# A scan in two sweeps: silu as one ScalarE instruction, and the first sweep moved behind the attention

## The chip, the cores and the metric

The kernel runs on one core of one Trainium2 chip. The metric is the device time of one execution in microseconds (us), given as the median of the runs shown. Everything is computed in fp32.

## The reference

What is computed, cut to what matters (T = 4096 rows x, S2 = 3202 rows of context, H = 512, 8 heads of 64, NS = 64 states):

```python
x1 = x + mha(layernorm(x), layernorm(ctx))       # 8 heads, softmax over 3202 keys
U  = (layernorm(x1) @ W_in.T + b_in) @ Bmat      # 4096 x 64

def step(s, u_t):
    s = silu(s @ A.T) + u_t
    return (s, s)
states = scan(step, zeros(64), U)                # 4096 steps, each on the one before

out = x1 + states @ Cmat + mean(program_probs) @ W_prog.T + b_prog
```

## The kernel before, in words

**Attention.** The 4096 queries are cut into 8 blocks of 512, each into 4 pairs of heads and 2 halves: 64 units. A unit goes through its keys in 13 steps of up to 256 keys. One step is a group of 16 scores matmuls (`scores`, L647), one exponential on ScalarE (`weights`, L724), one sum for the denominators on VectorE (`add`, L732) and a group of 16 matmuls with the values (`product`, L781). At a unit's end a "join" on VectorE (L830) empties the accumulator `o`, so that the next unit's first product can start. `sample`, `maximum`, `spread` and `base` find each unit's softmax reference beforehand. When a block is through, `project` does its output projection, the second layernorm, the transposing moves by DMA on SyncE's queue (`move`, L1010) and the input projection `pu` (L1109), whose result is kept in the tile `u`, as A's input for all time steps.

**How 4096 dependent steps are done.** The time axis is cut into 256 chunks of L = 16 steps. They lie side by side: 128 chunks on the upper 64 partitions, 128 on the lower ones, so one instruction does one step of all chunks. A first sweep (prefix `a`, in the trace the tile `za`) starts every chunk at zero and gives each chunk's end state, `end1`. A second sweep (prefix `b`, tile `z`) starts every chunk from its predecessor's `end1`; its states are the result. At the end `differ` compares the second sweep's end states with those of the first (bound `TOL` = 2^-21 of the largest), the number of differences is cast to an integer (`nbad`, L1703), and if it isn't zero a general path computes everything again with as many sweeps as are needed. The last 256 rows are ready only after the last unit; their scan is a separate one with chunks of 4 steps and 16 steps of run-up (`last_rows`, 20 small steps, tile `zl`).

**One step of a sweep** is, for each chunk, `z = A h + A u` and `h = silu(z)`; the state is `s = h + u`. TensorE makes the products with `u` four time steps at a time (`terms`, L1245), and adds A times `h` onto them (`z_`). Silu is made of two instructions: ScalarE's tanh (L1271) and VectorE's `(tanh + 1) z` (L1278); A is halved and `u` doubled beforehand so that no further factor is needed. The second sweep's state is added by GpSimd (`states`, L1310), from there TensorE takes it into `products` (L1317, into `py`), and `outputs` adds them to the rows: one half of the row block by VectorE (`joined`, L1337), the other, in two steps of three, by a ScalarE copy (L1331) and an addition on GpSimd (L1334), in the third by VectorE as well.

```python
        def tanh_(j):
            nc.scalar.activation(sv["th"][j % 2], at_(j), AF.Tanh, scale=0.5)
        ...
            nc.vector.scalar_tensor_tensor(
                h, sv["th"][j % 2], 1.0, at_(j), ALU.add, ALU.mult
            )
```

**What sets the order.** Each engine executes its instructions in one order that the program writes out. A planner (`Plan`) makes it: each piece has an engine, a cost, the pieces that it comes after, a due time in steps of 2150 ns, and rings of buffers that it takes and gives. Of the pieces that are ready the one due first goes next; `SHIFT` moves the due times of single kinds of pieces by hand. The first sweep is due within the last unit's steps (its z matmuls stand between scores and product groups, its tanh between the exponentials), `A_PACE` 1500 ns apart; the second sweep is due in the drain after the last unit, `B_PACE` 1900 ns apart. `drain` adds all of it, the last output projection (`last_products`, L1398) and the comparison.

Of the kernel before, what the change touches and what calls it, by code (L numbers as in the profile page):

```python
# [38 lines left out]
NP = 18  # L39
TOL = 2.0**-21  # L40
# [27 lines left out]
class Plan:  # L68
# [114 lines left out]
def xattn_ssm_kernel(  # L183
# [54 lines left out]
    bu2 = const.tile([P, 1], F32, name="bu2")  # L238
# [172 lines left out]
    def side():  # L411
# [65 lines left out]
        for k in (0, NS):  # L477
            nc.vector.tensor_copy(bu[k : k + NS], pb[:NS, 0:1])
            nc.vector.tensor_scalar(bu2[k : k + NS], pb[:NS, 0:1], 2.0, None, ALU.mult)
# [12 lines left out]
        nc.vector.tensor_scalar(a_t, a_t, 0.5, None, ALU.mult)  # L492
# [297 lines left out]
    def sums(w):  # L790

        if w["last"]:
            w["pd"] = ps_s.tile([P, 2, 512], F32, tag="s", name="pd_last")[:, 0, :QU]
# [38 lines left out]
    def finish(w, i, d, plan):  # L832
# [62 lines left out]
        if last:  # L895
            plan.add(("rise", i), "DVE", 480, rise, inverses, d + 9000, [], [("s", ("sums", i))])
# [134 lines left out]
    def project(plan, Q, halves, d, index):  # L1031

        for half in halves:
# [81 lines left out]
            def kept(t, w=w, at=at):  # L1115
# [6 lines left out]
                    bias=bu2[of],  # L1122
                    scale=2.0,
# [59 lines left out]
    A_PACE, B_PACE = 1500, 1900  # L1183
# [32 lines left out]
    def open_scan():  # L1216
# [7 lines left out]
        sv["th"] = [one[:, i, :] for i in range(2)]  # L1224
        sv["h"] = [one[:, 2 + i, :] for i in range(3)]
        sv["s"] = [one[:, 5 + i, :] for i in range(2)]
# [3 lines left out]
        for name, n in (  # L1230
            ("end0", NCK + 1), ("end1", NCK + 1), ("ul", PRE + 1 + P), ("hw", P), ("hl", P),
            ("sl", P + 1), ("df", NCK), ("thl", P // LT), ("st", P // LT),
# [12 lines left out]
    def terms(z, q, start):  # L1245

        if q:
            on_a(z, u[:, 4 * q - 1 : 4 * q + 3, :], start=True)
            return
        if start is not None:  # L1250
            on_a(z[:, 0, :], start, start=True)
        on_a(z[:, 1:, :], u[:, :3, :], start=start is None)

    def sweep(k, start, end, d=0, pace=0, after=()):

        def bank(q):
            return sv["za" if k == "a" else "z"][q % 2]

        def at_(j):
            return bank(j // 4)[:, j % 4, :]

        def terms_(q):
            terms(bank(q), q, None if start is None else sv[start][:, :NCK])

        def z_(j):
            on_a(at_(j), sv["h"][(j - 1) % 3], start=False)

        def tanh_(j):  # L1270
            nc.scalar.activation(sv["th"][j % 2], at_(j), AF.Tanh, scale=0.5)  # L1271

        def h_(j):
            h = sv["h"][j % 3]
            if j == 0 and start is None:
                nc.vector.memset(h, 0.0)
                return
            nc.vector.scalar_tensor_tensor(  # L1278
                h, sv["th"][j % 2], 1.0, at_(j), ALU.add, ALU.mult
            )  # L1280

        def last_():
            e = sv[end]
            nc.vector.tensor_tensor(e[:, 1:], sv["h"][(L - 1) % 3], u[:, L - 1, :], ALU.add)
            nc.vector.tensor_copy(e[NS:, 0:1], e[:NS, NCK : NCK + 1])

        for j in range(L):
            q = j // 4
            if j % 4 == 0:

                free = [(k, "h", 4 * q - 5)] if q > 1 else list(after)
                yield (k, "terms", q), "PE", 880, partial(terms_, q), free, d - 3 * pace if q else d, [], [], "quarters"
            if j or start is not None:
                if j:
                    yield (k, "z", j), "PE", 250, partial(z_, j), [(k, "terms", q), (k, "h", j - 1)], d, [], [], "quarters"
                yield (
                    (k, "tanh", j), "ACT", 280, partial(tanh_, j),
                    [(k, "z", j) if j else (k, "terms", 0)], d + 400,
                )
                free = [("states", j - 3)] if j > 2 and start is not None else []  # L1300
                gives = [("m", "open")] if k == "a" and j == L - 1 else []
                yield (k, "h", j), "DVE", 290, partial(h_, j), [(k, "tanh", j)] + free, d + 800, [], gives
            else:
                yield (k, "h", j), "DVE", 100, partial(h_, j), [(k, "terms", 0)], d + 800
            d += pace
        yield (k, "end"), "DVE", 450, last_, [(k, "h", L - 1)], d

    def states(j, h):
        s = sv["s"][j % 2]
        nc.gpsimd.tensor_tensor(s, h, u[:, j, :], ALU.add)  # L1310
        return s
# [10 lines left out]
    def outputs(j):  # L1322

        n = counts[1]
        spread = j % 3 < 2
# [4 lines left out]
        def copied():  # L1330
            nc.scalar.activation(sv["y"][:, j % 2, :], sv["py"][j % 2][1], AF.Copy, scale=0.5)  # L1331
# [4 lines left out]
        def joined(v):  # L1336
            nc.vector.scalar_tensor_tensor(  # L1337
                row(v), sv["py"][j % 2][v][: counts[v]], 0.5, row(v), ALU.mult, ALU.add
# [32 lines left out]
    def first_scan():  # L1371

        sv["za"] = [m_tile([P, 4, NCK], f"za_{k}") for k in range(2)]
# [15 lines left out]

    def ready_py():  # L1390

        yb = ps_s.tile([P, 2, H], F32, tag="s", name="py")
        sv["py"] = [None, [yb[:, v, :] for v in range(2)]]
# [9 lines left out]
    def last_rows(plan, d):  # L1403
# [45 lines left out]
        def kept_(g):  # L1449
            hs = slice(g * NS, (g + 1) * NS)  # L1450
            nc.vector.tensor_scalar(
                sv["ul"][hs, PRE + 1 :], v["pu"][g][hs], bu[hs], 2.0, ALU.add, ALU.mult
            )
# [40 lines left out]
        for g in range(2):  # L1494
            plan.add(("last", NC - 1, g), "PE", 950, partial(last_products, NC - 1, [g]),
                     [("scale", n, g), ("last", NC - 2)], d + g)
# [9 lines left out]
            plan.add(("l.inputs", g), "PE", 1050, partial(inputs_, g), [("l.copy", g)], d + g, mt)  # L1506
# [5 lines left out]
        plan.add("l.terms", "PE", 1100, terms_, [("l.kept", g) for g in range(2)], d, ["mt"], [], "quarters")  # L1512
        for t in range(PRE + LT):
            if t:
                plan.add(("l.z", t), "PE", 150, partial(on_, t), [("l.h", t - 1)], d, [], [], "quarters")
            plan.add(("l.tanh", t), "ACT", 180, partial(tanh_, t), [("l.z", t) if t else "l.terms"], d)
            plan.add(("l.h", t), "DVE", 180, partial(h_, t), [("l.tanh", t)], d)
# [11 lines left out]
    def last_output(g):  # L1529
        nc.vector.scalar_tensor_tensor(  # L1530
            xl[g], sv["pyl", g], 0.5, xl[g], ALU.mult, ALU.add
# [4 lines left out]
    def neighbours():  # L1536

        sl = sv["sl"]
        nc.vector.tensor_copy(sl[:NS, 0:1], sv["end0"][NS:, END : END + 1])
# [65 lines left out]
    def drain(plan):  # L1605
# [15 lines left out]
        plan.add("open", "DVE", 600, first_scan, ["c2", ("den", n - 4, 1), *kept_], a0, ["m", "m"])  # L1621
        for p in sweep("a", None, "end1", a0 + 1000, A_PACE, ["open"]):
            plan.add(*p)
        plan.add("start", "SP", 0, ready_scan, ["fetch", ("sums", n)], d - 2 * STEP, ["s"])
        plan.add("yb", "SP", 0, ready_rows, [("den", n - 1, 1)], a0, ["m", "m"])
        plan.add("py1", "SP", 0, ready_py, ["start", ("rise", n)], d, ["s"])
# [331 lines left out]
```

## Time and profile before

| | |
|---|---|
| median of 3 runs | 1967.35 us (1966.62 to 1969.19) |
| the profiled execution | 1969.03 us |
| its span | 1967.2 us |
| its mean granted TensorE clock | 0.995 |
| TensorE (PE) busy | 1930.5 us, 98% of the span |
| VectorE (DVE) busy | 1460.4 us, 74% |
| ScalarE (ACT) busy | 1174.3 us, 60% |
| GpSimd (POOL) busy | 225.1 us, 11% |

The profile is one execution of the program recorded by the hardware. The span goes from its first instruction to its last; the device time of the same execution is 1.8 us longer. L1243 is line 1243 of the kernel's file; a name such as `za<-u` is the tile that is written and the tile that is read. A row of the timeline begins with its time in the span and its duration in us; in brackets stands how long the engine was idle ahead of it and which engine ended that.

### The profile page before, as it was taken

How to read it: one execution, taken by the hardware profiler on the slowest of the kernel's cores; microseconds unless marked ns; L12 is line 12 of the kernel's file. 1: busy time of each engine (PE TensorE's matmuls, PEld its weight loads, DVE VectorE, ACT ScalarE, POOL GpSimd, SP SyncE). 2: the span in 40 equal slices, each digit the busy share in tenths (PEclk: the TensorE clock that was granted, in tenths of full speed). 3: DMA queues.
4: the chain of work that ended last, by engine and by line, in shares of the span. 5: the costliest groups of instructions: out<-in, count | busy, mean ns of one | idle time of the engine just before them, and what ended most of it. 6: DMA issues, size and time to landing. Idle time of an engine off the chain costs nothing. (4 is left out here: it accounts for less than half of the span.)

```text
span 1967.2 us, 66894 instructions
## 1 busy us (share of the span) xinstructions
PE 1930.5 (98%) x29070; PEld 1256.5 (64%) x29070; DVE 1460.4 (74%) x1977; ACT 1174.3 (60%) x1632; POOL 225.1 (11%) x378
## 2 busy tenths in 40 slices
PE   8999999999999999999999999999999999999997
PEld 4444577676666666666667666666666676766674
DVE  4221289688877887788868886888788886877776
ACT  2233377576666566666657665666666675665653
POOL 2111000001200120001100120012001110011105
PEclk9999999999999999999999999999999999999998
DMA  5632323223432243233412342224322331544475
GB/s 171 192 98 72 98 81 99 70 80 91 125 87 80 77 121 76 72 94 80 116 57 88 91 123 78 80 85 117 89 77 74 102 91 47 150 135 141 146 206 196
DMA packets 246933, 204.27 MB, mean 104 GB/s; under 512 B 80808, under 2 KB 220072, under 8 KB 246636
## 3 DMA queue, kind: packets, MB, share of 16 engines
q1 hardware_dynamic: 242088, 192.28, 34.1%
q10 hardware_dynamic: 4548, 7.67, 1.2%
q8 instruction: 230, 3.77, 0.8%
q14 instruction: 67, 0.55, 0.1%
HBM read 156.32 MB, written 29.88 MB: 95 GB/s over the span
## 5 line engine op out<-in xcount | busy, mean ns | idle before, releaser
L724 ACT ACTIVATE p<-s,shifts 128x1024 f32<-128x1024 f32 (+1 forms) x832 | 891.1, 1082 | 487.4 <-PE s L647 477.5
L732 DVE TENSOR_TENSOR acc<-p,acc 128x1024 f32<-128x1024 f32 (+1 forms) x704 | 830.7, 1180 | 205.5 <-ACT p L724 171.2
L647 PE MATMUL s<-q,k 64*64 64x256 f32 x12800 | 835.3, 377 | 5.6 <-ACT p L724 3.7
L781 PE MATMUL po<-p,v 64*64 64x256 f32 x12800 | 834.9, 377 | 3.0 <-DVE o L830 2.4
L647 PEld LDWEIGHTS s<-q,k 64*64 64x64 f32 x12800 | 490.2, 133 | 218.8 <-issue 17.0
L781 PEld LDWEIGHTS po<-p,v 64*64 64x64 f32 x12800 | 484.6, 133 | 194.1 <-issue 12.9
L1047 POOL TENSOR_TENSOR xr<-xr,rowb 128x512 f32<-128x512 f32 x30 | 42.9, 1440 | 988.1 <-DMA xr<-in_x_dram 854.0
L853 DVE RECIPROCAL rd<-rd 128x256 f32<-128x256 f32 (+1 forms) x64 | 110.2, 1722 | 12.9 <-ACT rd L848 12.5
L324 PE MATMUL pq<-xn,wq 128*128 128x512 f32 x256 | 113.9, 598 | 0.0
L1053 PE MATMUL pa<-wo,o 128*128 128x512 f32 x240 | 107.0, 599 | 0.0
L563 PE MATMUL pv<-wv,ct 128*128 128x512 f32 (+1 forms) x208 | 95.6, 612 | 1.0 <-ACT ct L531 0.7
L596 PE MATMUL pk<-ct,wk 128*128 128x512 f32 (+1 forms) x224 | 88.8, 549 | 0.0
L531 DVE COPY ct<-tp_c 128x512 f32<-128x512 f32 (+1 forms) x13 | 8.5, 651 | 104.5 <-PE tp_c L295 104.5
L732 DVE TENSOR_TENSOR acc<-p,p 128x1024 f32<-128x1024 f32 x64 | 78.2, 1221 | 9.0 <-ACT p L724 9.0
L324 PEld LDWEIGHTS pq<-xn,wq 128*128 128x128 f32 x256 | 47.3, 190 | 57.9 <-issue 56.7
L1053 PEld LDWEIGHTS pa<-wo,o 128*128 128x128 f32 x240 | 44.4, 190 | 56.0 <-issue 55.5
L756 DVE TENSOR_TENSOR acc<-swap,acc 64x256 f32<-64x256 f32 x126 | 62.7, 498 | 11.1 <-ACT swap L751 9.4
L563 PEld LDWEIGHTS pv<-wv,ct 128*128 128x128 f32 (+1 forms) x208 | 38.1, 192 | 44.4 <-issue 42.2
L596 PEld LDWEIGHTS pk<-ct,wk 128*128 128x128 f32 x224 | 39.2, 190 | 42.6 <-issue 42.6
L333 ACT ACTIVATE q<-pq,bias 128x512 f32<-128x512 f32 x32 | 22.0, 687 | 73.4 <-PE pq L324 73.4
L604 ACT ACTIVATE ks<-pk,bias 128x512 f32<-128x512 f32 (+1 forms) x28 | 18.0, 642 | 75.5 <-PE pk L596 68.4
L751 ACT COPY swap<-acc 64x256 f32<-64x256 f32 x126 | 50.8, 403 | 17.2 <-DVE acc L739 14.5
(213 smaller groups left out, 1203.3 us busy)
## 6 DMA issues: line engine op xcount, KB each, us to landing
k<-kd SPq DMA_DIRECT2D x432, 128.0 KB, 2.3
v<-vd SPq DMA_DIRECT2D x432, 128.0 KB, 2.3
xn<-x SPq DMA_DIRECT2D x416, 32.0 KB, 1.9
xr<-in_x_dram SPq DMA_DIRECT2D x30, 256.0 KB, 3.2
x1d<-xr SPq DMA_DIRECT2D x30, 256.0 KB, 2.2
x<-in_x_dram SPq DMA_DIRECT2D x28, 256.0 KB, 3.4
cx<-in_ctx_dram SPq DMA_DIRECT2D x25, 256.0 KB, 2.9
vd<-vs SPq DMA_DIRECT2D x25, 256.0 KB, 2.4
```

Source lines behind the costliest of these rows:

```text
L324: nc.tensor.matmul(pq, wq[:, i, hp * P : (hp + 1) * P], xn[:, i, :], start=(i == 0), stop=(i == NC - 1),)
L563: nc.tensor.matmul(pv[h * HD : h * HD + n, :H], ct[:, k, o : o + n], wv[:, k, :], start=(i == 0), stop=(i == NC // parts - 1), skip_group_ ...
L596: nc.tensor.matmul(pk[:, :n_g], wk[:, i, hp * P : (hp + 1) * P], ct[:, i, :n_g], start=(i == 0), stop=(i == NC - 1),)
L647: nc.tensor.matmul(s[k0 : k0 + HD, a, b, :], kts[(*w["at"][:2], c)][r, b * CK + k0 : b * CK + k0 + HD], q[r], start=True, stop=True, skip_ ...
L724: nc.scalar.activation(t[:, :, :nb, :], w["ps"][c][:, :, :nb, :], AF.Exp, bias=w["shift"])
L732: nc.vector.tensor_tensor(w["acc"][:, :, :nb, :], t[:, :, :nb, :], before[:, :, :nb, :], ALU.add)
L751: nc.scalar.copy(w["swap"][r], of[(1 - k) * HD : (2 - k) * HD])
L756: nc.vector.tensor_tensor(of[r], w["swap"][r], of[r], ALU.add)
L781: nc.tensor.matmul(w["po"][a * HD : (a + 1) * HD, k, :QU], vts[Q, hp, c][r, b, a * HD : (a + 1) * HD], t[r, a, b, :], start=(c == 0 and b ...
L853: nc.vector.reciprocal(w["rd"][:, part], (w["pd"] if last else w["rd"])[:, part])
L1047: nc.gpsimd.tensor_tensor(v["x"], v["x"], rowb, ALU.add)
L1053: nc.tensor.matmul(v["pa"], o_t[Q, c, half][:, t * P : (t + 1) * P], wo[:, c, :], start=(c == 0), stop=(c == NC - 1),)
```

## The change

Both sweeps take silu from ScalarE's own function: no tanh, no product on VectorE, and so neither a halved A nor a doubled `u`. Exponential and silu are not in one table of ScalarE, so the whole first sweep is moved behind the last exponential, with one table load between them. The first sweep keeps its terms products. The second sweep has none: its matmuls take the state itself (`z = A s`), silu is done in place in PSUM, and VectorE adds `u`, which gives the state; GpSimd's additions of the states go. The states lie in a ring of `HS` = 5 tiles. The rows of the lower half are spread over ScalarE and GpSimd at every step, where it was two of three. The scan of the last rows takes silu in the same way. The last output products are split by row tiles, two tiles in PSUM are shared, and `SHIFT` has new values, for pieces of the attention too.

```diff
+HS = 5
...
     SHIFT = {
-        "row.store": 16.5, "fold": 6.75, "rows.outs": 1, "heads": -12.25, "sample": -3, "spread": 5.75,
-        "query.flip": 10.25, "states": -11.5, "inverse": 7.5, "extra": 4, "scale": -13.25, "rest": 3.25,
-        "row.mod": -1.5, "joined0": -6,
+        "row.store": 19.5, "fold": 9.5, "rows.outs": 0.75, "heads": -12.25, "query.flip": 8.75, "start": -18.25,
+        "row.mod": -28.25, "add": -1, "spread": -2.75, "fall": 14.25, "query.stats": -16.25, "row.move1": 12.25,
+        "extra": 2.5, "last": -2.5, "gather": 9.5, "rest": 2.75, "row.load": -2, "join": -9.75, "differ": -1,
+        "row.stats": -3.75, "b": -35.75, "l.out": 10.25, "joined0": -6,
     }
...
-        nc.vector.tensor_scalar(a_t, a_t, 0.5, None, ALU.mult)
...
-                    bias=bu2[of],
-                    scale=2.0,
+                    bias=bu[of],
...
-    A_PACE, B_PACE = 1500, 1900
+    A_PACE, B_PACE = 850, 1900
...
+    def first_sweep(d, pace, after):
         def terms_(q):
+            if q:
+                on_a(sv["z"][q % 2], u[:, 4 * q - 1 : 4 * q + 3, :], start=True)
+            else:
+                on_a(sv["z"][0][:, 1:, :], u[:, :3, :], start=True)
         def z_(j):
+            if j > 1:
+                on_a(at_(j), sv["h"][(j - 1) % 2], start=False)
...
+            nc.scalar.activation(sv["h"][j % 2], at_(j), AF.Silu)
...
+            old = [("a", "h", j - 1)] if j > 1 else [("weights", len(units) - 1, NDC - 1)]
...
+    def sweep(start, d=0, pace=0, after=(), waits=lambda j: []):
+        def z_(j):
+            on_a(at_(j), sv["s"][(j - 1) % HS] if j else sv[start][:, :NCK], start=True)
+        def h_(j):
+            nc.scalar.activation(at_(j), at_(j), AF.Silu)
+        def states_(j):
+            nc.vector.tensor_tensor(sv["s"][j % HS], at_(j), u[:, j, :], ALU.add)
         for j in range(L):
+            yield ("b", "z", j), "PE", 220, partial(z_, j), [("states", j - 1)] if j else list(after), d, [], [], "quarters"
+            yield ("b", "h", j), "ACT", 280, partial(h_, j), [("b", "z", j)], d + 400
+            yield ("states", j), "DVE", 290, partial(states_, j), [("b", "h", j)] + waits(j), d + 800
...
-    def states(j, h):
-        s = sv["s"][j % 2]
-        nc.gpsimd.tensor_tensor(s, h, u[:, j, :], ALU.add)
-        return s
...
-        spread = j % 3 < 2
+        spread = j % 16 < 16
...
-        def tanh_(t):
-            nc.scalar.activation(sv["thl"], z_(t), AF.Tanh, scale=0.5)
         def h_(t):
-            nc.vector.scalar_tensor_tensor(hs_(t), sv["thl"], 1.0, z_(t), ALU.add, ALU.mult)
+            nc.scalar.activation(hs_(t), z_(t), AF.Silu)
...
-            plan.add(("last", c), "PE", 1900, partial(last_products, c),
-                     ["yb"] + [("scale", i, t) for t in range(2) if ("scale", i, t) in plan.pieces] + ([("last", c - 1)] if c else []), d + 8 * STEP + c)
+            for g in range(2):
+                scaled = ("scale", i, g if ("scale", i, g) in plan.pieces else 0)
+                plan.add(("last", c, g), "PE", 950, partial(last_products, c, [g]),
+                         [scaled, ("last", c - 1, g) if c else "yb"], d + 8 * STEP + c + g / 2)
```

More of the change, by code (lines that the diff above doesn't have):

```diff
@@ L1243, in on_a, with at_ @@
             nc.tensor.matmul(z[r], a_t[r, r], right[r], stop=True, skip_group_check=True, **how)
[L1245 to L1262, printed above, removed]
+    def at_(j):
+        return sv["z"][j // 4 % 2][:, j % 4, :]
@@ L1273, in h_ @@
         def h_(j):
[L1274 to L1280, printed above, removed]
+            nc.scalar.activation(sv["h"][j % 2], at_(j), AF.Silu)
         def last_():
-            e = sv[end]
-            nc.vector.tensor_tensor(e[:, 1:], sv["h"][(L - 1) % 3], u[:, L - 1, :], ALU.add)
+            e = sv["end1"]
@@ L1285, in last_ @@
+            nc.vector.tensor_tensor(e[:, 1:], sv["h"][(L - 1) % 2], u[:, L - 1, :], ALU.add)
             nc.vector.tensor_copy(e[NS:, 0:1], e[:NS, NCK : NCK + 1])
-        for j in range(L):
[L1288 to L1304, printed above, removed]
-            d += pace
@@ L1306, in sweep @@
-        yield (k, "end"), "DVE", 450, last_, [(k, "h", L - 1)], d
-    def states(j, h):
-        s = sv["s"][j % 2]
-        nc.gpsimd.tensor_tensor(s, h, u[:, j, :], ALU.add)
-        return s
+        for j in range(1, L):
+            q = j // 4
+            if j == 1 or j % 4 == 0:
+                free = [("a", "h", 4 * q - 5)] if q > 1 else list(after)
+                yield ("a", "terms", q), "PE", 860 if q else 650, partial(terms_, q), free, d - 3 * pace, [], [], "quarters"
+            old = [("a", "h", j - 1)] if j > 1 else [("weights", len(units) - 1, NDC - 1)]
+            if j > 1:
+                yield ("a", "z", j), "PE", 220, partial(z_, j), [("a", "terms", q)] + old, d, [], [], "quarters"
+            yield (("a", "h", j), "ACT", 280 if j > 1 else 1580, partial(h_, j),
+                   [("a", "z", j)] if j > 1 else [("a", "terms", 0)] + old, d + 400)
+            d += pace
@@ L1637, in drain, with waits @@
         last_rows(plan, d - 16 * STEP)
-        for p in sweep("b", "end1", "end0", d - 9 * STEP, B_PACE, [("a", "end"), "start"]):
+        def waits(j):
+            return [("products", j - HS, part) for part in range(2)] if j >= HS else []
+        for p in sweep("end1", d - 9 * STEP, B_PACE, [("a", "end")], waits):
             plan.add(*p)
```

86 lines of the change are left out of this document (38 added, 48 removed).

## The prediction

> **What bounds the kernel now.** I read the page, then windows cut at the places where the work changes character, then the tiles of the first sweep, then the timeline of the tail.
>
> ```profile
> span 1967.2 us, 66894 instructions
> PE 1930.5 (98%) x29070; PEld 1256.5 (64%) x29070; DVE 1460.4 (74%) x1977; ACT 1174.3 (60%) x1632; POOL 225.1 (11%) x378
> ```
>
> ```profile
> 1814.00:1817.40 3.40, 2.99 (x28) 2.34 (x32) 0.00 (x0) 0.95 (x2) 0.00 (x0) 0.50 0.81 241
> ...
> 1850.00:1907.00 57.00, 54.91 (x965) 43.19 (x965) 42.17 (x62) 36.49 (x59) 3.49 (x2) 1.00 0.59 161
> ...
> 1920.00:1951.30 31.30, 27.00 (x404) 19.18 (x402) 20.69 (x59) 14.61 (x44) 21.98 (x32) 1.00 0.56 185
> 1951.30:1967.20 15.90, 5.88 (x70) 2.95 (x62) 10.69 (x34) 2.07 (x7) 3.50 (x4) 0.69 0.61 210
> ```
>
> Columns: window, length, busy of PE, PEld, DVE, ACT, POOL, granted clock, DMA share, GB/s. Up to the last exponential (about 1907) TensorE sets the time: whatever it stops doing there is won one for one. After that nothing is full: from 1920 to 1951 the second sweep runs as a chain through three engines, and from 1951 to the end PE is busy 5.9 of 15.9 us. There latency and queue order count, not busy time. The profiled execution took 1969.03 us, 1.8 more than its span and 1.7 more than the median of 1967.35; I add my sum to 1969.03 and take 1.7 off for the median. The measurement can't tell less than 0.2% (3.9 us) from no change.
>
> **Before the last exponential: the first sweep goes.**
>
> ```profile
> L1243 PE MATMUL za<-scan,a_t x60: 269/269/320, 1857.6 to 1899.1; 64*64 64x128 f32 x60
> ...
> L1243 PE MATMUL za<-u,a_t x16: 482/589/589, 1856.0 to 1881.1; 64*64 64x512 f32 x12, 64*64 64x384 f32 x4
> ...
>   PEld za L1243: 1.5, 3
> ```
>
> ```profile
> 1867.23 0.59 PE L1243 MATMUL za<-u,a_t 64*64 64x512 f32 x1
> ...
> 1868.73 0.40 PE L781 MATMUL po<-p,v 64*64 64x256 f32 x2
> ...
> 1870.73 1.21 PE L647 MATMUL s<-q,k 64*64 64x256 f32 x16
> ...
> 1872.46 1.21 PE L647 MATMUL s<-q,k 64*64 64x256 f32 x16
> ...
> 1874.40 1.21 PE L647 MATMUL s<-q,k 64*64 64x256 f32 x16
> ```
>
> A scores group and a product group together advance TensorE 1.73 us (1870.73 to 1872.46), 0.865 each; with one step of the first sweep between them 1.94. So a step costs 0.21, and 60 matmuls are 15 steps: 3.2 us. A set of terms: from 1867.23 to 1868.73 (1.50 us) 14 of 16 product matmuls went out, worth 0.76, so the terms took 0.74; four sets, one at three quarters width, 2.8 us. Waits of the weight loads for VectorE's product 1.5. Together 7.4 us leave the bound stretch.
>
> **Also before it: the planner's order shifts.** The new SHIFT values move instructions everywhere; the number of changes between full and quarter tiles on TensorE stays. Three places in the old order stall and stand differently in the new one.
>
> ```profile
> 849.07 1.09 PE L781 MATMUL po<-p,v 64*64 64x256 f32 x16 [1.10 <-DVE o L830]
> ...
> 1270.97 1.09 PE L781 MATMUL po<-p,v 64*64 64x256 f32 x16 [1.09 <-DVE o L830]
> ...
> 1814.41 1.98 PE L1109 MATMUL pu<-xn,wc 128*64 128x128 f32 x16 [3.29 <-DMA xn<-x]
> ...
> 1850.01 1.09 PE L1109 MATMUL pu<-xn,wc 128*64 128x128 f32 x16
> ```
>
> At 1811 the input projection of the block at row 3328 waits 3.29 us for its transposing moves, and then the clock is at 0.50 from 1814 to 1817.4: 2.99 busy us do 1.5 us of work (its 16 matmuls take 1.98 instead of 1.09). In the new order two scores groups and a product stand ahead of it, 3 x 0.865 = 2.6 us. On SP's queue the last of its four moves goes behind one more k load, one more v load and two row loads, but a k and a v load go ahead of the first move, into SP's idle time; I take the landing as unchanged. The stall shrinks to 0.7, and the half clock should go: 2.6 + 1.5 = 4.1 us won (bounds 0 and 4.8). The page "TensorE: Matmul & The Clock Gate" of the Trainium skill (Part 1) states that the clock halves after an idle window of about 3.4 us; the trace agrees, with 3.29 idle and 3.4 at half. By that rule 0.7 idle keeps the clock; if the halving came all the same, the place would give 2.6.
>
> At 849 and 1271 the next unit's first product waits for the join that empties its accumulator. In the new order 0.43 us more of other matmuls stand between, and the join is due 9.75 steps earlier on VectorE: 2.2 us won (bounds 0.9 and 2.2). Against that, the softmax maxima have less time: the least distance between sample and spread falls from 2.4 to 1.7 us of TensorE work at two places. No row prices that; between 0 and one more stall like that at 1811 (3.29 + 1.5), nearest to the 1.1 us rows, I take 1.5 lost. Sum up to the last exponential: -7.4 - 4.1 - 2.2 + 1.5 = -12.2 us.
>
> **After it: the first sweep comes back, serial.**
>
> ```profile
> 1906.62 0.70 ACT L724 ACTIVATE p<-s,shifts 128x512 f32<-128x512 f32 x1
> ...
> 1911.40 3.70 PE L1398 MATMUL yb<-wo,o 128*128 128x512 f32 x8
> ...
> 1916.05 3.77 PE L1398 MATMUL yb<-wo,o 128*128 128x512 f32 x8
> ...
> 1919.75 0.43 PE L1243 MATMUL z<-scan,a_t 64*64 64x128 f32 x4
> ...
> 1922.23 0.81 ACT L279 ACTIVATE xh_yl<-x_l,nmr_yl,rstd_yl 128x512 f32<-128x512 f32 x1 [0.15 <-POOL nmr_yl L271]
> ...
> 1922.62 0.43 PE L1243 MATMUL z<-scan,a_t 64*64 64x128 f32 x4 [0.93 <-DVE scan L1278]
> ...
> 1923.10 0.28 ACT L1271 ACTIVATE scan<-z 128x128 f32<-128x128 f32 x1
> 1923.41 0.29 DVE L1278 SCALAR_TENSOR_TENSOR scan<-scan,z 128x128 f32<-128x128 f32 x1 [0.85 <-ACT scan L1271]
> ...
> 1923.75 0.20 PEld L1243 LDWEIGHTS z<-scan,a_t 64*64 64x64 f32 x4 [0.94 <-DVE scan L1278]
> ```
>
> ```profile
> 3.67 1.28 ACT L279 ACT_TABLE_LOAD   x1 [3.67 <-DMA cx<-in_ctx_dram]
> ```
>
> Times here are on the old clock, with the last exponential at 1906.62. A link of the chain: PE to ACT 0.48, ACT to DVE 0.31, DVE to PE 0.34. Silu drops the middle engine: a step of the first sweep is 0.48 + 0.34 = 0.82 us where nothing stands between. Silu needs one table load, which this trace shows at 1.28 us; the program has one, behind the last exponential, and Copy and Identity need no other. The first silu can start at 1908.6.
>
> The order on TensorE then is: terms and steps z2 to z7 between the last products and the output projection, z8 behind the whole projection of the last rows. Work from 1906.4 to z8: terms 2.0, products 4.3, sums 1.0 (estimate: eight 256-wide matmuls at full tile), steps 1.3, projection 7.5: 16.1, so z8 at 1922.5. The table load lies beside this (step 7 is ready some 5 us before), and so costs nothing; were that cover gone it would cost its 1.28. From z8: eight steps 6.6, terms 0.7, two row scalings on ScalarE ahead of steps 9 and 11 (0.81 each) 1.6, transposes, copies and input projection of the last rows ahead of z14 and z15 2.7, the end state on VectorE 0.5: 12.1. The second sweep starts at 1934.6, not 1919.75: 14.9 later.
>
> ```profile
> 1932.64 0.29 DVE L1278 SCALAR_TENSOR_TENSOR scan<-scan,z 128x128 f32<-128x128 f32 x1 [0.22 <-POOL scan L1310]
> ...
> 1936.10 0.60 ACT L1331 ACTIVATE y_l<-py 128x512 f32<-128x512 f32 x1 [0.28 <-POOL row L1334]
> ...
> 1936.73 0.69 DVE L1337 SCALAR_TENSOR_TENSOR row<-py,row 128x512 f32<-128x512 f32 x1 [0.50 <-ACT y_l L1331]
> 1936.77 1.28 POOL L1334 TENSOR_TENSOR row<-y_l,row 112x512 f32<-112x512 f32 x1 [0.24 <-PE zl L1243]
> ...
> 1950.99 0.28 DVE L1278 SCALAR_TENSOR_TENSOR scan<-scan,z 128x128 f32<-128x128 f32 x1
> ```
>
> Old pace, outputs running: 11 steps from 1932.64 to 1950.99, 1.67 each. New work a step: GpSimd 1.28 (one row add each step, no states), TensorE 0.865 + 0.21 + 0.1 = 1.2, ScalarE 0.28 + 0.60 and a small silu of the last rows 0.2, 1.1, VectorE 0.29 + 0.69, 1.0. The chain alone is 0.48 + 0.31 + 0.34 = 1.13. So 1.28 is the floor and 1.67 the old pace; I take 1.45, since the old order lost about a quarter over its fullest engine and the new one has one VectorE step less. Fifteen steps 21.8 and the first 1.1: the last state at 1957.5, 6.2 later than the old 1951.3.
>
> ```profile
> 1952.10 0.29 DVE L1356 TENSOR_REDUCE scan<-scan 128x1 f32<-128x128 f32 x1
> ...
> 1955.09 0.15 DVE L1369 TENSOR_SCALAR scan<-scan 128x1 f32<-128x1 f32 x1
> ...
> 1959.38 0.61 DVE L1492 TENSOR_TENSOR scan<-scan 128x128 f32<-128x128 f32 x1
> ...
> 1963.42 0.14 DVE L1703 CAST nbad<-py 1x1 int32<-1x1 f32 x1
> ```
>
> Behind the last state the old kernel needs 12.3 us to 1963.6, because the last rows' scan trails. In the new one it goes without VectorE and one step beside each step of the second sweep, so it is done with it. What is left is VectorE's: the comparison 3.1 (1952.10 to 1955.24), last states to the end 4.2 (1959.38 to 1963.56), and two row joins that now stand behind the comparisons, 1.4: 8.7. End at 1966.2, against 1963.6: +2.6. Total -12.2 + 2.6 = -9.6: 1959.4 on the profiled execution, 1958 at the median.
>
> **The rivals.**
> No change that can be measured: TensorE loses only the 7.4 of the sweep, the stalls move elsewhere, and the second sweep keeps 1.67 (15 x 0.22 = 3.3 more): -7.4 + 2.6 + 3.3 = -1.5, 1966. For it: other stalls of a reordered program can't be read in a trace of the old one.
> Slower: each step of the second sweep waits in three in-order queues behind the previous row's output work: z behind 0.865 of products, silu behind a 0.60 copy, state behind a 0.69 join. All of it gives 1.13 + 2.15 = 3.3 a step. From -9.6 to +3.9 it decides at 1.45 + 13.5 / 15 = 2.35 a step; at 2.5 it gives 1974. Against it: the old order, with more on VectorE, ran 1.67.
> Clock: from z9 to z15 TensorE does little but wait, and in the old tail the granted clock falls to 0.69 on average. A halving of 3.4 us costs at most 1.7; two, one there and one in the second sweep, give 1961. By the rule of the same page of the skill, PE idle for a window in the drain brings it.
> Better: stalls elsewhere go too and the sweep runs at its floor: -1.5 - 2.6 more, 1954 or less.
> The change doesn't do what it says: the kernel compares both sweeps to 2^-21 and redoes everything if they differ. Old sweeps rounded alike; the new second one rounds h + u before the product, the first doesn't. One entry beyond the bound adds milliseconds.
>
> **How the numbers follow.** Forecast 0.48, clock 0.12, better 0.11, no change 0.16, slower by queues 0.06, by a new TensorE stall like that at 1811 in several blocks 0.04, by the fallback 0.03. So faster by over 0.2% 0.71, within 0.2% 0.16, slower 0.13. Range: below, better than the floor case with all old stalls gone, 1950; above, the no-change case and a little, 1967.
>
> **What would show it.** No za in the stretch 1850 to 1907, which ends about 12 us earlier; no 0.50 clock at the 3328 block; one table load of 1.28 behind the last exponential; second sweep starting some 28 us behind the last scores; its states 1.3 to 1.6 us apart; 8 to 9 us from its last state to the cast. Wrong if TensorE shows new idle of several us before the last exponential, if states are over 2 us apart, or if the fallback's lines run.

## The result, and the profile after

The changed kernel takes 1974.32 us (median of 7 runs, 1970.49 to 1976.24), the kernel before 1966.83 (7 runs): ratio 1.0033, 95% interval 1.0021 to 1.0045. It is slower by 0.33%, where 1958 was forecast; the number lies outside the range of 1950 to 1967. The profiled execution took 1974.32 us with a span of 1972.5, 5.3 more than before.

Where the 5.3 us come from is read along one kind of instruction that both kernels have at the same point of the work: the 512-wide exponential that ends a unit. From ScalarE's timeline, first of before, then of after (start, duration, engine, line, operation):

```profile
1793.97 0.69 ACT L724 ACTIVATE p<-s,shifts 128x512 f32<-128x512 f32 x1
...
1852.62 0.69 ACT L724 ACTIVATE p<-s,shifts 128x512 f32<-128x512 f32 x1 [0.36 <-PE s L647]
```

```profile
1800.40 0.69 ACT L723 ACTIVATE p<-s,shifts 128x512 f32<-128x512 f32 x1
...
1856.96 0.69 ACT L723 ACTIVATE p<-s,shifts 128x512 f32<-128x512 f32 x1
...
1903.05 0.70 ACT L723 ACTIVATE p<-s,shifts 128x512 f32<-128x512 f32 x1
1903.76 1.28 ACT L1261 ACT_TABLE_LOAD   x1
1905.05 0.28 ACT L1261 ACTIVATE scan<-z 128x128 f32<-128x128 f32 x1
```

The changed kernel is 6.4 us late at 1800.40, before anything of the scan has run; 4.3 late at 1856.96, behind the block at row 3328; and 3.6 ahead at the last exponential (1906.62 before). The stretch that lost the sweep gave 7.9 us. From the last exponential to the end of the span it takes 69.45 us instead of 60.58: 8.9 lost.

The first 6.4 us are waits of TensorE in the attention, one or two in nearly every block. TensorE's timeline of after:

```profile
429.04 1.96 PE L780 MATMUL po<-p,v 64*64 64x256 f32 x32 [1.59 <-DVE o L831]
...
638.51 2.10 PE L646 MATMUL s<-q,k 64*64 64x256 f32 x32 [1.22 <-ACT p L723]
...
852.70 1.96 PE L780 MATMUL po<-p,v 64*64 64x256 f32 x32 [0.95 <-DVE o L831]
...
1064.81 1.96 PE L780 MATMUL po<-p,v 64*64 64x256 f32 x32 [1.07 <-DVE o L831]
...
1276.48 1.96 PE L780 MATMUL po<-p,v 64*64 64x256 f32 x32 [0.95 <-DVE o L831]
...
1488.46 1.96 PE L780 MATMUL po<-p,v 64*64 64x256 f32 x32 [0.95 <-DVE o L831]
...
1700.29 2.10 PE L646 MATMUL s<-q,k 64*64 64x256 f32 x32 [1.20 <-ACT p L723]
...
1822.55 1.35 PE L1110 MATMUL pu<-xn,wc 128*64 128x128 f32 x16 [2.41 <-DMA xn<-x]
```

In brackets stands the wait and who ended it: mostly the join on VectorE (L831 after, L830 before). At 638 and 1700 it is an exponential, which stands in ScalarE's queue behind a copy that itself waited 2.1 us for an addition on VectorE. What VectorE does ahead of the join at 429, and GpSimd beside it, from their timelines:

```profile
422.40 2.19 DVE L731 TENSOR_TENSOR acc<-p,p 128x1024 f32<-128x1024 f32 x1
424.62 1.81 DVE L717 TENSOR_TENSOR acc<-x,acc 2x256 f32<-2x256 f32 x2
426.54 1.23 DVE L731 TENSOR_TENSOR acc<-p,acc 128x1024 f32<-128x1024 f32 x1
427.69 0.84 DVE L755 TENSOR_TENSOR acc<-swap,acc 64x256 f32<-64x256 f32 x2
428.56 0.42 DVE L831 TENSOR_TENSOR o<-po,o 128x256 f32<-128x256 f32 x1
...
422.07 3.66 POOL L1048 TENSOR_TENSOR xr<-xr,rowb 128x512 f32<-128x512 f32 x2 [106.46 <-DMA k<-kd]
```

Two additions and a gather stand ahead of the join. The first addition takes 2.19 us and the pair of small ones 1.81, while GpSimd adds the row of biases to the row block (`xr`, 3.66 for two, where each takes 1.27 with nothing beside it). The same instructions without that neighbour are shown below, with the run without row additions: 1.22 and 0.84.

### The profile page after: what moved, and what is told of

Its sections match the earlier page's. It is cut to its first block, busy times and chain, and to the rows that moved or that the text cites. A ratio compares the mean times of both kernels' runs of the same rounds, so it can differ in the third digit from the quotient of the medians.

```text
span 1972.5 us, 66769 instructions
## 1 busy us (share of the span) xinstructions
PE 1930.2 (98%) x29050; PEld 1245.6 (63%) x29050; DVE 1455.7 (74%) x1931; ACT 1174.7 (60%) x1638; POOL 232.6 (12%) x367
## 4 chain that ended last, share of the span: by engine, by line
## 5 line engine op out<-in xcount | busy, mean ns | idle before, releaser
L646 PEld LDWEIGHTS s<-q,k 64*64 64x64 f32 x12800 | 482.0, 133 | 223.1 <-ACT p L723 21.2
L755 DVE TENSOR_TENSOR acc<-swap,acc 64x256 f32<-64x256 f32 x126 | 53.6, 426 | 14.1 <-ACT swap L750 12.5
```

Of the source, the lines that this page charges most:

```text
L646: nc.tensor.matmul(s[k0 : k0 + HD, a, b, :], kts[(*w["at"][:2], c)][r, b * CK + k0 : b * CK + k0 + HD], q[r], start=True, stop=True, skip_ ...
L755: nc.vector.tensor_tensor(of[r], w["swap"][r], of[r], ALU.add)
```

## The experiments

Ratios are to the kernel before, run on the same chip, with 95% intervals. "Row additions" are the two of GpSimd just shown; those at a block boundary belong to the first half of a block's output projection.

**The order and the scan, apart.** The attention's SHIFT values go back to the old ones in the changed kernel, and into the kernel before the new ones.

```diff
-        "row.store": 19.5, "fold": 9.5, "rows.outs": 0.75, "query.flip": 8.75, "row.mod": -28.25, "add": -1, ...
+        "row.store": 16.5, "fold": 6.75, "rows.outs": 1, "sample": -3, "spread": 5.75, "inverse": 7.5, ...
```

> The changed kernel, with the old SHIFT values for the pieces of the attention; the pieces of the drain keep the new ones. Theory (the new order of the attention costs time in every block: VectorE does the second add and the gather ahead of the join, and TensorE waits for the join): the 6.4 us of stalls that built up to 1794 are gone, the old 3.3 us wait at the projection of row 3328 is back (2.1 us lost against the new order), so the last exponential ends about 4.3 us earlier than in the changed kernel and the time is about 1970.0. Rival (the loss comes with the moved sweep and the drain alone, the attention's order is neutral): 1974, as the changed kernel.

> The kernel before, with the new SHIFT values for the pieces of the attention; scan and drain as before. Theory: the stalls come with the order alone, +6.4 up to the block at row 3328, -2.1 there, so about +4.3 on 1966.8: 1971. Rival: they need the changed drain or scan, and it stays at 1967.

Measured: 1967.0 us, ratio 0.9994 (0.9984 to 1.0004), and 1975.34, ratio 1.0035 (1.0023 to 1.0046). So the new scan alone makes no difference that can be told, and the new order alone makes the kernel before as slow as the changed one. The theory holds, and both effects are larger than the 4.3 us it gave: 7.7 and 6.9 us by the ratios.

**What in the order.** One kernel takes the gather away from the join, the other nearly takes GpSimd's row additions away.

```diff
-        "fold": 9.5, ..., "gather": 9.5, ...
+        "fold": 6.75, "inverse": 7.5, ...
```

> The changed kernel with three SHIFT values of VectorE's end of a unit as before (fold 6.75, gather none, inverse 7.5); gather then stands ahead of the second of the next unit's adds instead of right ahead of the join, the join keeps its place behind that add. Theory that the place of the gather in VectorE's queue makes the join late: the stalls at the block boundaries go from about 1.4 to about 0.5 us each, the time falls by 3 to 4, 1970.5. Rival (the number of instructions ahead of the join counts, not which, and the collisions with GpSimd's row additions add 1 us each): within 1 us of 1974.

```diff
-                nc.gpsimd.tensor_tensor(v["x"], v["x"], rowb, ALU.add)
+                nc.gpsimd.tensor_tensor(v["x"][:, :8], v["x"][:, :8], rowb[:, :8], ALU.add)
```

> The changed kernel, where GpSimd adds the row of biases to 8 of 512 columns of each row block only (504 columns of that addition are left out), so that its two additions of 1.3 us at each block boundary are nearly gone. Theory that GpSimd's additions hold up VectorE at the same time (the second add took 2.19 there instead of 1.21 us, the rest 1.81 for two instead of 0.84, the fold 1.63 instead of 0.67): these durations return to their medians, the waits for the join at 429, 1065, 1488 and for the exponential at 638 and 1700 go, and the time falls by 4 to 6, to about 1969. Rival (place in the queue alone): the long durations stay or the waits stay, less than 1 us.

Measured: 1976.74, ratio 1.0047 (1.0032 to 1.0063), with a wait of 0.91 or 0.92 us for the join at each of six block boundaries; and, without the row additions, 1960.7, ratio 0.9959 (0.9945 to 0.9973). Moving the gather wins nothing back, so its place alone is not the cause. Without the row additions no wait over 0.5 us is left between 231 and 1800. VectorE's timeline there, the same five instructions:

```profile
422.31 1.22 DVE L731 TENSOR_TENSOR acc<-p,p 128x1024 f32<-128x1024 f32 x1
423.57 0.84 DVE L717 TENSOR_TENSOR acc<-x,acc 2x256 f32<-2x256 f32 x2
424.52 1.23 DVE L731 TENSOR_TENSOR acc<-p,acc 128x1024 f32<-128x1024 f32 x1
425.66 0.85 DVE L755 TENSOR_TENSOR acc<-swap,acc 64x256 f32<-64x256 f32 x2
426.54 0.42 DVE L831 TENSOR_TENSOR o<-po,o 128x256 f32<-128x256 f32 x1
```

The queue is the same, the join comes 4.23 us behind the first addition's start instead of 6.16. The 1.93 us are some 0.97 twice, in the two instructions beside GpSimd's additions. The Trainium skill's page "SBUF — State Buffer" (section "SBUF: two separate sides") says that VectorE, in an instruction with two inputs in SBUF, and GpSimd share one pair of ports, which the one that starts first holds to the end of its instruction. The durations here agree with that.

**The same without leaving work out.** The row block's loads at the boundary start four steps later, so that the additions run behind the join. The second kernel combines the run without additions with the old order.

```diff
+            early = 6 if half else 2
...
-                         [(*ks[0], "load")] if t else [from_(d - 6 * STEP)], d - 6 * STEP + t, ...
+                         [(*ks[0], "load")] if t else [from_(d - early * STEP)], d - early * STEP + t, ...
```

> The changed kernel, where the row block's loads of the first half of a project start 4 steps (about 7 us) later, so that GpSimd's two additions of the biases at a block boundary run behind the join and not ahead of it; VectorE's order at the join is the same and all work is done. Theory (the stalls come from GpSimd's additions holding up VectorE ahead of the join): the waits at 429, 638, 853, 1065, 1276, 1488 and 1700 go or fall below 0.5 us, and the time falls by 6 to 9 from 1974, to about 1967. Rival (what the run without the additions gained, it gained elsewhere, or the additions now hold up the running adds as much): 1973 to 1975.

> The changed kernel with the old order of the attention, and GpSimd's additions of the biases on 8 of 512 columns only (504 are left out). Theory that the order costs only through those additions: it stands within 2 us of the new order without them (1960.7). Rival (the new order costs by itself too): lower by 4 or more, 1956; or, if the new order is better by itself and only suffers from them, above 1963.

> The kernel before with the row loads at the block boundaries 4 steps later, nothing else. Theory (the old order suffers little from GpSimd's additions: its waits of 1.1 us at 849 and 1271 and 0.85 at 1697 go): 2 to 3 us faster, ratio 0.9985, so most of the 15 us that the same edit gave the changed kernel is peculiar to the new order. Rival (the additions cost the old order as much, and the edit is a gain by itself): ratio 0.993.

Measured: the changed kernel with later loads 1959.12, ratio 0.9948 (0.9931 to 0.9964); the old order without additions 1963.0, ratio 0.9963 (0.9952 to 0.9975); and the kernel before with later loads 1969.38, ratio 1.0011 (1.0001 to 1.0020). The first is the strongest result: with all work done, and VectorE's order at the join as it was, the changed kernel falls from 0.33% above to 0.52% below the kernel before. Its waits of 0.5 us or more between 231 and 1890:

```profile
1552.29 1.96 PE L780 MATMUL po<-p,v 64*64 64x256 f32 x32 [0.50 <-DVE o L831]
...
1758.44 1.09 PE L1111 MATMUL pu<-xn,wc 128*64 128x128 f32 x16 [0.54 <-DMA xn<-x]
...
1807.42 1.09 PE L1111 MATMUL pu<-xn,wc 128*64 128x128 f32 x16 [1.20 <-DMA xn<-x]
```

It gained more than the 6 to 9 us expected: its last exponential starts 14.4 us sooner than in the changed kernel, at 1888.66, of which 12.2 were won before row 3328 and 2.2 there, where the wait shrank from 2.41 to 1.20. The waits of TensorE that the profiles show account for some 8 of the 12.2; what made the rest is not shown. The additions still meet VectorE's sums, but behind the join, which ends at 427.3 here:

```profile
427.26 5.80 DVE L731 TENSOR_TENSOR acc<-p,acc 128x1024 f32<-128x1024 f32 x3
...
428.48 3.50 POOL L1048 TENSOR_TENSOR xr<-xr,rowb 128x512 f32<-128x512 f32 x2 [112.57 <-DMA xr<-in_x_dram]
```

Three sums take 5.80 us, 1.9 more than three without that neighbour, and TensorE does not wait for them. So it is the place of the meeting that costs, not the meeting. Without the additions, old and new order stand at 0.9963 and 0.9959: the order costs only through them. They cost the old order too, which stands at 0.9994 with them. The third missed both its expectations. The old order's waits for the join did go, but other small ones came (0.70 at 1084, 3.70 instead of 3.29 at row 3328, in an execution of 1975.24, the slowest of the ten). The edit is no gain by itself; it pays where the additions stand in the way of a join.

**The drain: clock.** Four pairs of idle matmuls between steps 9 and 13 of the first sweep, on the old order.

```diff
+            if 9 < j < 14:
+                yield ("a", "fill", j), "PE", 400, fill_, [("a", "z", j - 1)], d - pace, [], [], "quarters"
...
+        def fill_():
+            on_a(sv["py"][1][1][:, :256], u[:, :2, :], start=True)
```

> The changed kernel with the old order of the attention, and four pairs of idle 256-wide matmuls between the steps 9 to 13 of the first sweep, which write into a bank that nothing reads then. Theory (TensorE works only half of the time from step 9 to 13, and the granted clock of 0.50 that follows for some 6 us costs the transposes, copies and projection of the last rows about 2.5 to 3 us): no 0.50 clock ahead of the second sweep, whose first step comes 2.5 us sooner behind the last exponential, time about 1964.5 against 1967. Rival (the slow part waits for ScalarE and GpSimd, not for TensorE's clock, or the end is set by something else): 1966 to 1968.

Windows of the changed kernel first, where steps 9 to 13 run from 1922.76 to 1926.9, then of the run with fillers (length, busy of PE, PEld, DVE, ACT, POOL, granted clock, DMA share, GB/s):

```profile
1923.00:1925.00 2.00, 1.06 (x12) 0.39 (x8) 0.00 (x0) 1.41 (x4) 1.82 (x4) 1.00 0.02 6
1925.00:1927.00 2.00, 1.20 (x9) 0.59 (x10) 0.00 (x0) 0.60 (x3) 1.62 (x2) 0.66 0.34 130
1927.00:1929.00 2.00, 2.00 (x10) 1.67 (x12) 0.00 (x0) 0.96 (x3) 0.00 (x0) 0.50 0.35 132
1929.00:1931.00 2.00, 2.00 (x15) 1.67 (x14) 0.00 (x0) 0.76 (x2) 0.00 (x0) 0.50 0.00 0
1931.00:1933.00 2.00, 2.00 (x19) 1.59 (x17) 1.07 (x4) 0.12 (x1) 0.00 (x0) 0.63 0.00 0
```

```profile
1917.00:1919.00 2.00, 1.99 (x22) 0.82 (x16) 0.00 (x0) 1.41 (x5) 1.84 (x3) 1.00 0.00 0
1919.00:1921.00 2.00, 1.99 (x19) 1.17 (x18) 0.00 (x0) 0.71 (x3) 1.45 (x2) 1.00 0.35 131
1921.00:1923.00 2.00, 2.00 (x23) 1.66 (x22) 0.04 (x1) 1.25 (x3) 0.00 (x0) 1.00 0.35 131
```

With TensorE busy half of the time the clock halves, just ahead of the transposes and the projection; with fillers, whose steps 9 to 13 run from 1916.6 to 1920.5, it stays at 1.00. Measured from the end of the last exponential, the second sweep's first silu stands at 28.15 us with fillers, at 29.58 in the same kernel without, and at 30.85 in the changed kernel, whose half clock lasted longest (6.8 us, against 3.4). So the stretch costs 1.4 to 2.7 us, by how long the halving lasts. The time was 1964.88, ratio 0.9979 (0.9970 to 0.9989), against 0.9994: the 1.4 us are in the profile, the two ratios' intervals still overlap.

**The drain: table load.** The second set of terms goes ahead of the first silu in TensorE's queue, on the kernel with later row loads.

```diff
-                yield ("a", "terms", q), "PE", 860 if q else 650, partial(terms_, q), free, d - 3 * pace, ...
+                yield ("a", "terms", q), "PE", 860 if q else 650, partial(terms_, q), free, d - (40 if q == 1 else 3) * pace, ...
```

> The changed kernel with the later row loads, and the second set of terms ahead of the first silu in TensorE's queue, so that it does not wait there for a silu that waits for the table load. Theory (the load isn't covered: TensorE waits 0.96 us for the first silu, with the last products queued behind it): that wait goes, and step 8 of the first sweep comes 0.8 to 1.0 us sooner, 17.7 instead of 18.7 us behind the last exponential. Rival (the wait is hidden by the wait for the last exponential's products anyway): step 8 within 0.3 us of 18.7.

In the changed kernel this row of TensorE's timeline shows what it waits for:

```profile
1905.38 0.65 PE L1242 MATMUL z<-u,a_t 64*64 64x512 f32 x2 [0.96 <-ACT scan L1261]
```

Measured (one execution, 1958.24): step 8's silu 17.86 us behind the end of the last exponential instead of 18.69, the second sweep 0.82 sooner. The load is not covered: the second set of terms writes the other half of the tile that the first silu reads, so it waits for that silu, and the last products stand behind it.

**The drain: which end.** The last output products come later, the first sweep's steps between them.

```diff
-        "extra": 2.5, "last": -2.5, ...
+        "extra": 2.5, "last": 8, ...
```

> The changed kernel with the later row loads, and the due time of the last output products 10.5 steps later, so that the steps 8 to 11 of the first sweep stand between them and not behind them; the last rows' transposes and projection come later for that. Theory (the second sweep and the last rows' scan are two chains of about one end, 54.1 and 56.2 us behind the last exponential): the second sweep starts some 4 us sooner, the last rows' scan ends some 2 to 5 us later, and the end moves by the later one: 1961 to 1964. Rival (the second sweep alone sets the end): 1955.

Measured: 1958.65, ratio 0.9956 (0.9941 to 0.9971) against 0.9948; neither expected time came. The second sweep starts 4.6 us sooner (25.15 behind the last exponential instead of 29.72), the last rows' scan ends 4.1 later (60.3 instead of 56.2), the cast 2.3 later. But the second sweep also ran slower, 2.0 us a step instead of 1.6, and its last state came 1.4 later (55.6 instead of 54.2). So starting it sooner gained nothing here; which of the two chains sets the end, this run can't tell.

**The drain: pace of the second sweep.** Three edits of the place of ScalarE's copy in the odd steps: ahead of VectorE's addition (`joined0` waits for `copied`), behind the next silu, and behind the silu after that. The diff is the third.

```diff
+                if sort == "copied" and j % 2 and j + 2 < L:
+                    more = more + [("b", "h", j + 2)]
```

> The changed kernel with the old order of the attention, and in the odd steps of the second sweep ScalarE's copy ahead of VectorE's addition, which both read the one tile py. Theory (ScalarE's copy stands behind VectorE's addition for that tile, and the next silu behind the copy, which makes two steps take 3.29 us): two steps in 2.6 to 2.8 us, the last state 3.5 to 4.5 us sooner, time about 1963. Rival (GpSimd's two additions of 1.25 and its wait for the copies set the pace, or VectorE's addition, now behind the copy, delays the next state as much): two steps in 3.2 or more, 1967.

> The changed kernel with three edits: the row loads at the block boundaries 4 steps later, the four pairs of idle matmuls in the first sweep, and in the odd steps of the second sweep ScalarE's copy of py behind the next step's silu (VectorE's addition stays ahead of it). Theory (the two readers of the one tile py make the next silu wait behind the copy, some 0.7 us in each pair of steps): two steps in 2.6 to 2.8 us, last state 49 us behind the last exponential instead of 54, and with the 1.4 us of the filler the time is about 1953 where the kernel before takes 1969.6. Rival (with silu ahead, the copy comes later and GpSimd's two additions or the last rows, one step beside each step, hold the pace at 3.1 or more): 1957 to 1958.

> The changed kernel with the later row loads, and in the odd steps of the second sweep ScalarE's copy of py behind the silu two steps later (the silu that stood behind it until now); VectorE's addition stays ahead of the copy. Theory (the pace of 1.64 a step comes from a silu that waits in ScalarE's queue behind a copy, which waits for VectorE's addition, since both read one tile): two steps in 2.5 to 2.8 us instead of 3.29, the last state 49 to 50 us behind the last exponential instead of 54.1. Rival (GpSimd's additions, 2.5 us for two plus its wait for the copies, hold the pace): 3.1 us or more, 53 to 54.

Two steps of the changed kernel, from the timelines of VectorE, ScalarE and GpSimd:

```profile
1944.47 0.69 DVE L1323 SCALAR_TENSOR_TENSOR row<-py,row 128x512 f32<-128x512 f32 x1 [0.31 <-PE py L1303]
...
1945.25 0.59 ACT L1317 COPY y_l<-py 128x512 f32<-128x512 f32 x1 [1.27 <-DVE row L1323]
1945.73 0.27 ACT L1288 ACTIVATE z<-z 128x128 f32<-128x128 f32 x1
...
1945.91 2.50 POOL L1320 TENSOR_TENSOR row<-y_l,row 112x512 f32<-112x512 f32 x2 [0.78 <-ACT y_l L1317]
...
1949.20 2.52 POOL L1320 TENSOR_TENSOR row<-y_l,row 112x512 f32<-112x512 f32 x2 [0.79 <-ACT y_l L1317]
```

The copy waits for VectorE's addition, as both read the tile `py`, and the silu, whose z was there at 1944.73, stands behind the copy: 3.29 us for two steps. With the copy ahead of the addition (1965.07, ratio 0.9977, 0.9967 to 0.9986) two steps took 3.12 and the last state came no sooner (54.10 instead of 54.01): now VectorE's next state stood behind its addition. What this run gained came behind the last state: the last rows' scan was done 7.7 us sooner, their two additions on VectorE no longer stood behind the comparisons, and the span ended 2.0 us sooner. Its ratio's interval still overlaps that of 0.9994. The second edit left ScalarE's order as it was, and with it the pace, so that its run (1956.3, ratio 0.9945, 0.9933 to 0.9957) tells only of the filler: the second sweep starts 1.6 us sooner, and the ratio can't be told from the 0.9948 without it. The third:

```profile
1926.54 0.27 ACT L1289 ACTIVATE z<-z 128x128 f32<-128x128 f32 x1
...
1925.90 2.51 POOL L1321 TENSOR_TENSOR row<-y_l,row 112x512 f32<-112x512 f32 x2 [0.20 <-ACT y_l L1318]
1928.62 2.52 POOL L1321 TENSOR_TENSOR row<-y_l,row 112x512 f32<-112x512 f32 x2 [0.21 <-ACT y_l L1318]
```

2.72 us for two steps, of which GpSimd works 2.51: its floor of 1.28 a step is nearly reached. The last state stands 51.9 us behind the last exponential instead of 54.1 (49 to 50 was expected), since the last five steps run slower than the others. One execution took 1954.7. Its span ends 4.0 us sooner behind the last exponential than with the later loads alone, 2.3 of it by the last state.

**All together**: later row loads, fillers, early terms, late copy.

> The changed kernel with the later row loads, the four pairs of idle matmuls in the first sweep, the second set of terms ahead of the first silu, and the late copy. What the single edits gave: 1.4 (filler) and 0.8 (terms) ahead of the second sweep, and 4 to 5 in it if the theory of the copy holds: about 1952 to 1953 where the kernel before takes 1968.7, ratio 0.992. Rival (the pace stays): 1956, ratio 0.994.

Measured: 1952.95, ratio 0.9917 (0.9902 to 0.9931). It beats both kernels, by 0.8% and by 1.2%; the cast stands 57.8 us behind the last exponential, with the later loads alone 62.6, in the changed kernel 63.7.

## Why the prediction was wrong

**The first sweep** was forecast at -7.4 and measured at -7.9 (4.34 late at 1856.96, 3.57 ahead at 1903.05). The mechanism is right; that the size fits to 0.5 us is partly luck. Between the same two exponentials, kernels of one order that differ in the scan differ by 9.5 us (before against changed kernel with the old order) and by 6.7 (before with the new order against changed kernel).

**The planner's order** is the step that failed: -2.2 for two joins and +1.5 for new stalls, together -0.7, and +6.4 was measured. The two joins at 849 and 1271 were not won: they still cost 0.95 us each, at 852.70 and 1276.48. The prediction took the join's due time, 9.75 steps earlier, for its place; the join comes after the copy of the unit's finished products (`output`), so it could not be ready then, and in VectorE's written order two additions and mostly the gather stood ahead of it. That alone would have been harmless, as the runs without row additions and with later loads show. The waits came from GpSimd's row additions, of which the sum had no term; they run when their load lands, and now fell on two-input additions ahead of the join. The kernel held a hint: in its planner's reckoning a GpSimd piece never runs beside VectorE's `add`, `rest`, `fold`, `gather` or `scale` (the tuple `PORT`); in the trace they meet. The rival "a new TensorE stall in several blocks" was near to what happened, and had 0.04.

**The block at row 3328** was forecast at -4.1 and gave 2.1 (6.43 late at 1800.40, 4.34 at 1856.96). The wait went from 3.29 to 2.41 and not to 0.7, and the half clock stayed. The 2.6 us of work ahead of the projection came as forecast: TensorE runs dry 19.7 us behind the exponential at 1800.40, before 17.1 behind the one at 1793.97. Both other reasons of the step failed: the moves' landing, taken as unchanged, came later, and a shorter wait did not keep the clock. On SyncE's queue the four moves go out until 20.6 us behind that exponential, before until 18.8, as two row loads now stand ahead of them. First before, then after:

```profile
1810.21 2.52 SPq L1010 DMA_DIRECT2D xn<-x  x4
```

```profile
1817.51 0.42 SPq L1045 DMA_DIRECT2D xr<-in_x_dram  x1
1817.98 3.00 SPq L1011 DMA_DIRECT2D xn<-x  x4
```

The wait and the clock behind it, after (windows as above):

```profile
1820.10:1822.50 2.40, 0.04 (x4) 0.00 (x0) 2.37 (x3) 1.47 (x2) 1.02 (x2) 1.00 0.38 87
1822.50:1824.00 1.50, 1.45 (x20) 1.15 (x24) 1.47 (x2) 0.07 (x1) 0.63 (x1) 0.75 0.83 260
1824.00:1825.80 1.80, 1.80 (x20) 1.09 (x24) 0.67 (x1) 0.90 (x2) 0.00 (x0) 0.50 0.78 245
```

**After the last exponential**, +2.6 was forecast and +8.9 measured. Counted from the start of the last exponential, the second sweep began at 30.8 and not at 28.0. Its step 8 came 2.1 us late, at 18.0 instead of 15.9: 0.8 is the table load's, which the prediction had at nothing, and the rest lies in the work ahead of it. From there to the second sweep it took 12.9 instead of 12.1, with 2.7 lost to the half clock, which the prediction had as a rival with 0.12 and at most 1.7 for one place. Without that loss it would have been 1.9 shorter than forecast: the row scalings, put at 1.6, lengthened no step, as steps 8 to 12 are 0.87 us apart. So two errors there nearly cancel, which is luck.

The second sweep's pace, from first state to last, was 1.61 and not 1.45, 2.4 us over 15 steps; the prediction looked for a full engine and missed that two readers of one tile take turns. From the end of the last state to the end of the cast it took 8.3 us against 8.7: right in size. But the last rows' scan was not done with the second sweep, as forecast: its last silu ends 2.1 us behind the last state. In the run with the copy first, where it is done before, the cast came 1.0 us sooner. From the cast to the end of the span 5.0 us instead of 3.8: SyncE still issues a row store, until 1967.81, before it can read the count, which is 0.4 of the 1.2; what made the rest is not shown. The prediction named the two joins behind the comparisons, but not the store behind the joins:

```profile
1966.98 0.35 SPq L1508 DMA_DIRECT2D out_dram<-xr_l  x1
1967.39 0.42 SPq L1328 DMA_DIRECT2D out_dram<-row  x1
1967.47 0.14 DVE L1679 CAST nbad<-py 1x1 int32<-1x1 f32 x1
```

**The rivals.** Slower through three in-order queues, from 2.35 us a step, did not come: 1.61, near the old pace of 1.67 that the rival of no change had. The fallback did not run.

Together: 7.1 in the order, 2.0 at row 3328, -0.5 in the sweep and 6.3 behind the last exponential make the 14.9 between -9.6 and +5.3.

## What to carry to other kernels

Read a reordered program in the written queue of each engine, not in its due times, and lay the instructions of GpSimd beside VectorE's two-input instructions in time: what starts when a DMA lands has a time that no queue's order tells. A step that is moved to where TensorE is half empty can pay in clock, here 1.4 to 2.7 us, and two readers of one tile that take turns act as one more queue. Where an order costs, ask which neighbour makes it cost before going back to the old one: here four steps on a load turned +0.33% into -0.52%.

## What the runs showed of the hardware that was not expected

The clock halved behind idle stretches of 2.41 us (changed kernel) and 2.59 (old order), and stayed at 1.00 behind 2.39 (without row additions) and 3.04 (before with new order). It also halved behind some 3.3 us (1922.3 to 1925.6 in the changed kernel) in which TensorE worked half of the time and never paused longer than 0.44 us. The Trainium skill's page "TensorE: Matmul & The Clock Gate" (Part 1) has the gate watch a window of about 3.4 us that runs on its own and throttle behind an idle one. That a wait of 2.41 us costs and one of 3.04 doesn't agrees with a window that runs on its own. But all four waits are shorter than the window, so it need not be idle throughout; the half-busy stretch shows the same. What share of busy time keeps the clock stays open.

Beside GpSimd's two additions at 422 in the changed kernel, which took 3.66 us together where each takes 1.27 alone, VectorE's additions of two SBUF tensors took 0.97 us longer, twice (2.19 instead of 1.22, and 1.81 instead of 0.84 for a pair). The table load cost 1.30 us from the end of the last exponential to the first silu.
